# Decoder block on one core: cross-attention's maxima, sums and subtractions in three chains of VectorE instead of one; exponentials placed between product steps; value steps ahead of key steps

## The chip, the cores and the metric

The kernel runs on one core of a Trainium2 chip. Its time is the device time of one execution in microseconds (us). Three executions gave 1714.55, 1710.16 and 1714.2 us, median 1714.2. The engines are named as the profile names them: PE is TensorE (PEld its weight loads), ACT is ScalarE, DVE is VectorE, POOL is GpSimd, SP is SyncE, which issues the DMAs here. Each engine runs its own instructions in the order in which the program issues them, and waits for the others through semaphores.

## The reference

One decoder layer in float32: self-attention, cross-attention to a context of 750 rows, and a gated feed-forward network with quantised weights, each followed by an addition and a layer norm. The change touches the cross-attention alone:

```python
# x: (8, 224, 512), context: (8, 750, 384), 16 heads of 64
q = split_heads(x @ Wq); k = split_heads(context @ Wk); v = split_heads(context @ Wv)
sim = jnp.einsum('bhid,bhjd->bhij', q, k) * SCALE
attn = jax.nn.softmax(sim, axis=-1)          # over the 750 context rows
out = jnp.einsum('bhij,bhjd->bhid', attn, v)
out = out.transpose(0, 2, 1, 3).reshape(b, sq, HEADS * DIM_HEAD) @ Wo + bo
```

The softmax needs, for each head and query, the maximum over 750 scores, the exponentials of the scores less that maximum, and their sum.

## The kernel before

The self-attention fills the first 490 us of the profile or so, the feed-forward network the last 160. Between them the cross-attention runs in 32 **turns** (the loop at line 1408, `for t in range(-1, TURNS)`). A turn is four heads of one batch element. Two batch elements share eight turns: turns 2g and 2g+1 of the eight take the same four heads of the first and of the second element, so query projections come once for two turns, at the end of the odd one. After eight turns the output projection of the two elements follows.

**Layout.** Scores are held transposed: 125 context rows on the partitions, in six tiles (`NCT`), and 224 queries along the free axis. Heads come in two pairs, `w` = 0 and 1; tile `cpT0` or `cpT1` (`pT`) holds the two heads `j` of a pair, 125 x 6 x 224 each. A maximum or a sum over context rows is thus first one over the six tiles, elementwise, and then one across partitions.

**What a turn t issues, in order:**

1. `weighted(t-1)` (line 1326): 48 matmuls, the values of the turn before times its exponentials, into `ov_c`; a copy by ACT to `ov_s`.
2. `reduce_kind(quarter, 1)` (line 1249): DVE reduces `csm`, the partial sums of the exponentials of turn t-1, with a transposing reduction (line 1251).
3. `scores(t)` (line 1211): 48 matmuls (line 1227) into PSUM tiles, 12 copies by ACT to `cpT0`, then `cpT1` (line 1235). As the copies land, DVE takes the maxima over tiles: four tensor-tensor instructions a pair (`cm`, line 1237) and a last one into the region `mx` (line 1241; the profile calls the region by the name of its buffer, `xw`).
4. `across` (line 1256): one chain on DVE for both pairs and for maxima and sums at once. It reduces `mx` (line 1251), copies four partition groups of 32 side by side (`mx_s`, line 1268), reduces to negative maxima (line 1275) and to sums (line 1281), takes the reciprocals of the sums (line 1285) and copies the results to the other partition groups (`mx_n`, three copies, line 1292).
5. `less_maxima(0)` (line 1297): a transposition spreads the negative maxima of pair 0 over the partitions, into the PSUM tile `mx_b` (line 1300); two tensor-tensor instructions, one a head, add them to `cpT0` (line 1307).
6. The projections of the keys for turn t+1 and of the values for turn t, `kv_steps` (line 1167). Each is a generator over `half_steps` (line 1101), which computes the product from seven half-size block products with sums taken beforehand. It has eight steps: PE multiplies, ACT copies the accumulator (a snapshot `m1`, `u2`, `u4`, or a finished block), POOL adds two blocks (lines 1121 and 1140), and in step 7 DVE adds the last (`ckT` or `cv`, line 1148). An accumulator goes on being written after its snapshot is copied. The steps alternate: key 1, value 1, key 2 and so on up to 5; between them stands `weight_work`, the rounding of the feed-forward weights.
7. `exponentials(0)` (line 1316): for each head one ACT instruction (line 1319) and three additions of POOL that sum the six tiles to `csm` (lines 1322 to 1324).
8. Key 6, value 6, `less_maxima(1)`, key 7 and 8, value 7 and 8.
9. `normalise(t-1)` (line 1345): DVE spreads the reciprocals (line 1350) and multiplies `ov_s` into `coT` (line 1360).
10. In odd turns, `query_steps(t+1)` with eight steps of its own; among them `exponentials(1)`, the first head after step 1, the second after step 5.
11. After eight turns, output projections of finished tokens (`mm_co`, line 262) in turns 7, 8, 15, 16, 23, 24 and 31 and behind the loop, transpositions of the next inputs in turns 6, 14 and 22, and sums of the next context by POOL at the ends of turns 6, 7, 14, 15, 22 and 23 (lines 708 and 1074).

The order within each engine is the order of the program text, written out by hand (`manual_schedule`). All tiles named here have one buffer, except `mx_n` with two; PSUM tiles of the tag `mm` have six, handed out in the order in which they came free. SP issues the loads of the blocks of weights and contexts; the change moves none of them.

## Time and profile before

| what | us |
|---|---|
| median of three runs | 1714.2 |
| the profiled execution, whole | 1714.3 |
| its span, first to last instruction | 1712.5 |
| mean granted clock of PE | 0.981 |
| PE idle from 492 to 1556 us of the span (windows over the stage) | 75 |

Turns are read from the trace by the first score product (line 1227) of each. An even turn with neither projection nor transpositions takes 24.8 to 27.2 us (turn 18: 1097.85 to 1122.81, PE busy 24.09 of it). An odd one takes 34.4 to 36.9 (turn 19: 1122.81 to 1157.17, PE busy 30.53), and 29.2 where the turn before held a projection. Eight plain pairs of an even and an odd turn (2-3, 4-5, 10-11, 12-13, 18-19, 20-21, 26-27, 28-29) take 59.1 to 63.0 us, 60.6 on average. The pairs that hold an output projection of two tiles (8-9, 16-17, 24-25) take 66.8 each, and PE is never idle in them.

The page's groups give a line, the engine, the operation, the tile written and those read, the shape, the count, then the time busy and the mean of one in ns, then the engine's idle time just ahead of the group and what ended it. A row of the timeline gives the start and the length in us, the engine, the line, and how often the instruction came in a row.

### The profile page before, as it was taken

How to read it: one execution, taken by the hardware profiler on the slowest of the kernel's cores; microseconds unless marked ns; L12 is line 12 of the kernel's file. 1: busy time of each engine (PE TensorE's matmuls, PEld its weight loads, DVE VectorE, ACT ScalarE, POOL GpSimd, SP SyncE). 2: the span in 40 equal slices, each digit the busy share in tenths (PEclk: the TensorE clock that was granted, in tenths of full speed). 3: DMA queues.
4: the chain of work that ended last, by engine and by line, in shares of the span. 5: the costliest groups of instructions: out<-in, count | busy, mean ns of one | idle time of the engine just before them, and what ended most of it. 6: DMA issues, size and time to landing. Idle time of an engine off the chain costs nothing.

```text
span 1712.5 us, 26691 instructions
## 1 busy us (share of the span) xinstructions
PE 1619.5 (95%) x9682; PEld 1152.9 (67%) x9682; DVE 1339.9 (78%) x2388; ACT 1005.8 (59%) x1874; POOL 962.6 (56%) x861
## 2 busy tenths in 40 slices
PE   8999999999999999989998989988989999989998
PEld 5677666677657777866877756876866877754443
DVE  4999887799937677766678766888986788866877
ACT  5676554566426756745766735766764556545663
POOL 5885566565435646654645674464586456461244
PEclk9999999999999999999999999999999999999999
DMA  8115234243032222321212322322330111112433
GB/s 282 56 61 190 84 122 130 87 128 102 22 134 74 69 69 71 97 89 47 91 55 88 114 83 64 106 85 72 108 109 30 40 35 37 67 50 77 70 82 105
DMA packets 143108, 149.10 MB, mean 87 GB/s; under 512 B 41089, under 2 KB 109185, under 8 KB 142593
## 3 DMA queue, kind: packets, MB, share of 16 engines
q1 hardware_dynamic: 142976, 147.40, 28.3%
q8 instruction: 76, 1.25, 0.3%
q14 instruction: 56, 0.45, 0.1%
HBM read 119.85 MB, written 18.87 MB: 81 GB/s over the span
## 4 chain that ended last, share of the span: by engine, by line
PE 62%; DVE 20%; issue 7%; POOL 6%; ACT 4%; DMA 0%; POOLq 0%; DVEq 0%; SPq 0%; ACTq 0%
PE mm_f L1512 5%; PE mm_co L262 5%; PE ov_c L1335 5%; PE mm_v L544 5%; PE q_x L470 5%; PE mm_o L669 5%; PE sc_c L1227 4%; DVE cpT L1307 4%; DVE cm L1237 3%; PE k_x L1083 3%; POOL csh L1322 3%; PE ov_a L640 3%; PE v_x L1089 3%; PE sc_a L571 3%; PE q_w L470 2%
## 5 line engine op out<-in xcount | busy, mean ns | idle before, releaser
L1322 POOL TENSOR_TENSOR csh<-cpT 125x672 f32<-125x672 f32 x128 | 214.8, 1678 | 92.8 <-DVE cpT L1307 85.7
L1319 ACT ACTIVATE cpT<-cpT 125x1344 f32<-125x1344 f32 x128 | 168.0, 1325 | 97.2 <-DVE cpT L1307 92.5
L200 POOL TENSOR_TENSOR nm_i<-nm_q,mhalf 128x28 f32<-128x28 f32 x32 | 157.9, 4936 | 81.8 <-DVE nm_q L519 81.4
L1307 DVE TENSOR_TENSOR cpT<-cpT,mx_b 125x1344 f32<-125x1344 f32 x128 | 193.2, 1551 | 6.6
L1235 ACT COPY cpT<-sc_c 125x448 f32<-125x448 f32 x384 | 170.6, 592 | 11.5 <-PE sc_c L1227 11.0
L1227 PE MATMUL sc_c<-cq,ckT 64*125 64x224 f32 x1536 | 162.8, 360 | 10.8 <-ACT cpT L1235 10.5
L1227 PEld LDWEIGHTS sc_c<-cq,ckT 64*125 64x125 f32 x1536 | 147.2, 185 | 25.8 <-ACT cpT L1235 12.6
L1335 PE MATMUL ov_c<-cpT,cv 125*64 125x224 f32 x1536 | 155.6, 357 | 7.4 <-DVE cv L1148 7.4
L1121 POOL TENSOR_TENSOR ckT<-ckT,xwq 128x375 f32<-128x375 f32 x32 | 35.5, 1108 | 210.7 <-ACT ckT L1120 210.7
L1335 PEld LDWEIGHTS ov_c<-cpT,cv 125*64 125x64 f32 x1536 | 107.2, 137 | 53.3 <-DVE cv L1148 11.5
L1237 DVE TENSOR_TENSOR cm<-cpT 125x448 f32<-125x448 f32 x128 | 91.9, 759 | 29.3 <-ACT cpT L1235 26.0
L1251 DVE TRANSPOSE_TENSOR_REDUCE mx_r<-csm 128x28 f32<-128x896 f32 x32 | 35.5, 1108 | 91.8 <-POOL csm L1324 91.8
L262 PE MATMUL mm_co<-xattn_Wo,coT 128*128 128x512 f32 x224 | 100.1, 604 | 4.8 <-DVE coT L1360 4.8
L1512 PE MATMUL mm_f<-ternary,xqT 128*128 128x512 bf16 x448 | 98.8, 379 | 1.7 <-DVE x L1373 0.9
L544 PE MATMUL mm_v<-wv,xnT 128*128 128x512 f32 x224 | 100.4, 592 | 0.0
L1096 PE MATMUL mq_x<-xwq 128*128 128x224 f32 x192 | 55.3, 419 | 42.4 <-ACT xwq L1114 41.8
L1323 POOL TENSOR_TENSOR csm<-csh 125x224 f32<-125x224 f32 x128 | 89.0, 696 | 10.0
L282 ACT ACTIVATE pr<-sc_a 128x448 f32<-128x448 f32 x120 | 57.9, 535 | 60.4 <-PE sc_a L571 60.1
L1324 POOL TENSOR_TENSOR csm<-csm,csh 125x224 f32<-125x224 f32 x128 | 85.0, 664 | 10.0
L1237 DVE TENSOR_TENSOR cm<-cpT,cm 125x448 f32<-125x448 f32 x128 | 87.0, 720 | 0.0
L595 DVE TRANSPOSE_TENSOR_REDUCE sm_q<-pr 128x28 f32<-128x896 f32 x64 | 70.6, 1103 | 19.3 <-ACT pr L282 18.9
L1140 POOL TENSOR_TENSOR ckT<-ckT,cku 128x375 f32<-128x375 f32 x32 | 32.6, 1020 | 94.3 <-ACT cku L1139 94.3
(232 smaller groups left out, 3944.9 us busy)
## 6 DMA issues: line engine op xcount, KB each, us to landing
w_slot<-qk_sums SPq DMA_DIRECT2D x22, 512.0 KB, 3.6
xw<-w_sums SPq DMA_DIRECT2D x32, 320.0 KB, 2.9
xwq<-xq_sums SPq DMA_DIRECT2D x16, 512.0 KB, 4.0
w_stage<-w_gateT SPq DMA_DIRECT2D x16, 512.0 KB, 4.5
w_stage<-w_upT SPq DMA_DIRECT2D x16, 512.0 KB, 4.3
w_stage<-w_downT SPq DMA_DIRECT2D x16, 512.0 KB, 3.7
tern<-w_t SPq DMA_DIRECT2D x24, 256.0 KB, 2.5
ternary<-tern SPq DMA_DIRECT2D x3, 2048.0 KB, 7.7
```

Of the source, the lines that this page charges most:

```text
L200: nc.gpsimd.tensor_tensor(y, v, mhalf.to_broadcast([P, v.shape[-1]]), ALU.pow)
L262: nc.tensor.matmul(mm, lhsT=oT[:, k, c : c + P], rhs=w[:, k, :], start=(k == 0), stop=(k == NPAIR - 1),)
L470: nc.tensor.matmul(mm, lhsT=w[:, k], rhs=c[:, k], start=start and k == 0, stop=True, skip_group_check=True,)
L544: nc.tensor.matmul(mm, lhsT=xnT[:, k, at : at + P], rhs=wv[:, k, c * 512 : (c + 1) * 512], start=(k == 0), stop=(k == KD - 1),)
L1227: nc.tensor.matmul(sc[j][:, i, :], lhsT=kT[h0 : h0 + DH, w, ct * CT : (ct + 1) * CT], rhs=q[h0 : h0 + DH, t % 2, w], start=True, stop=True,)
L1235: nc.scalar.copy(pT[:, j, 2 * c2 : 2 * c2 + 2, :], sc[j])
L1237: nc.vector.tensor_tensor(m2[:, j], pT[:, j, 2 * c2 : 2 * c2 + 2, :], pT[:, j, 0:2, :] if c2 == 1 else m2[:, j], ALU.max,)
L1307: nc.vector.tensor_tensor(pT[:, j], pT[:, j], nm[:CT, j] .rearrange("p (o q) -> p o q", o=1) .to_broadcast([CT, NCT, S]), ALU.add,)
L1319: nc.scalar.activation(pT[:, j], pT[:, j], AF.Exp)
L1322: nc.gpsimd.tensor_tensor(half, pT[:, j, 0:3], pT[:, j, 3:6], ALU.add)
L1335: nc.tensor.matmul(ov[h0 : h0 + DH, w, :], lhsT=v[:, ct, hq * DH : (hq + 1) * DH], rhs=pTs[w][:, j, ct, :], start=(ct == 0), stop=(ct == N ...
L1512: nc.tensor.matmul(mm, lhsT=xqTs[i][:, k, :], rhs=w[:, k, cols], start=(k == 0), stop=(k == KD - 1),)
```

## The change

The chain for four heads is taken apart into three: one for the sums (`sum_inverses`), one each for the maxima of pair 0 and of pair 1 (`maxima`). The sums are reduced to their reciprocals right after `weighted`, ahead of the scores. The maxima over tiles leave `scores`; `maxima(pTs[0])` and `less_maxima` of pair 0 come after all scores, then `maxima(pTs[1])`. `mx` shrinks to two heads and serves both pairs. Value steps come ahead of key steps; the exponentials of pair 0 stand after steps 2 and 3 of the two products, ahead of the snapshots of step 3 (`u2`) and of the copies of step 4; `weight_work`'s two middle parts follow step 5. `less_maxima` of pair 1 comes after value step 7 and ahead of key step 7, and the exponentials of pair 1 after value step 8 and after query step 1. The last key step stands ahead of `normalise` in odd turns, and behind the last exponential in even ones.

```diff
@@ -840,8 +840,8 @@
                 n_xw = 2 * (KC + 2 + NSUM) * P
                 xw = xw_all[:, :n_xw].rearrange("p (j i n) -> p j i n", j=2, n=P)
                 bo = xw_all[:, n_xw : n_xw + DIM]
-                mx = xw_all[:, n_xw + DIM : n_xw + DIM + 4 * S].rearrange(
-                    "p (j q) -> p j q", j=4
+                mx = xw_all[:, n_xw + DIM : n_xw + DIM + 2 * S].rearrange(
+                    "p (j q) -> p j q", j=2
                 )
                 open_context(0, ctx_even)
                 load_context(0)
@@ -1214,7 +1214,6 @@
             pTs = []
             for w in range(2):
                 pT = sb.tile([CT, 2, NCT, S], F32, name=f"cpT{w}")
-                m2 = sb.tile([CT, 2, 2, S], F32, name="cm2")
                 for c2 in range(NCT // 2):
                     sc = [
                         ps_mm.tile([CT, 2, S], F32, tag="mm", name=f"sc_c{j}")
@@ -1233,76 +1232,66 @@
                             )
                     for j in range(2):
                         nc.scalar.copy(pT[:, j, 2 * c2 : 2 * c2 + 2, :], sc[j])
-                        if c2 > 0:
-                            nc.vector.tensor_tensor(
-                                m2[:, j], pT[:, j, 2 * c2 : 2 * c2 + 2, :],
-                                pT[:, j, 0:2, :] if c2 == 1 else m2[:, j], ALU.max,
-                            )
-                nc.vector.tensor_tensor(
-                    mx[:CT, 2 * w : 2 * w + 2], m2[:, :, 0, :], m2[:, :, 1, :], ALU.max
-                )
                 pTs.append(pT)
             return pTs
 
-        NH = 4 * NB
-
-        def reduce_kind(quarter, k):
-            y, op = ((mx, ALU.max), (csm, ALU.add))[k]
+        def across(y, n, op, name):
+
+
+            quarter = sb.tile([P, n * NB], F32, name=f"{name}_r")
             nc.vector.tensor_reduce(
-                quarter[:, k], y.rearrange("p j (b c) -> p (j b) c", c=Q32), AX.X, op,
+                quarter, y.rearrange("p j (b c) -> p (j b) c", c=Q32), AX.X, op,
                 apply_transpose=True,
             )
-
-        def across(quarter, first, last):
-
-
-
-
-            kinds = slice(1 if last else 0, 1 if first else 2)
-
-            if not last:
-                reduce_kind(quarter, 0)
-
-            side = sb.tile([Q32, 2, NH, P // Q32], F32, name="mx_s")
+            side = sb.tile([Q32, n * NB, P // Q32], F32, name=f"{name}_s")
             for g in range(P // Q32):
+                nc.vector.tensor_copy(side[:, :, g], quarter[g * Q32 : (g + 1) * Q32])
+            return side
+
+        def sum_inverses():
+
+            side = across(csm, 4, ALU.add, "sm")
+            tot = sb.tile([Q32, 4, NB], F32, name="sm_t")
+            nc.vector.tensor_reduce(
+                tot.rearrange("p j b -> p (j b)"), side, AX.X, ALU.add
+            )
+            res = sb.tile([P, 2, 2, NB, 1], F32, name="sm_n", bufs=2)
+            for j in range(2):
+                nc.vector.reciprocal(res[:Q32, j, :, :, 0], tot[:, j::2])
+            for g in range(1, P // Q32):
                 nc.vector.tensor_copy(
-                    side[:, kinds, :, g], quarter[g * Q32 : (g + 1) * Q32, kinds]
-                )
-
-
-            res = sb.tile([P, 12, NB, 1], F32, name="mx_n", bufs=2)
-            if not last:
-                nc.vector.tensor_reduce(
-                    res[:Q32, 2:6, :, 0].rearrange("p j b -> p (j b)"), side[:, 0], AX.X,
-                    ALU.max, negate=True,
-                )
-            if not first:
-                tot = sb.tile([Q32, 4, NB], F32, name="mx_t")
-                nc.vector.tensor_reduce(
-                    tot.rearrange("p j b -> p (j b)"), side[:, 1], AX.X, ALU.add
-                )
+                    res[g * Q32 : (g + 1) * Q32, g // 2, :, :, 0],
+                    res[:Q32, g // 2, :, :, 0],
+                )
+            return res
+
+        def maxima(pT):
+
+            m2 = sb.tile([CT, 2, 2, S], F32, name="cm2")
+            for c2 in range(1, NCT // 2):
                 for j in range(2):
-                    nc.vector.reciprocal(res[:Q32, 6 * j : 6 * j + 2, :, 0], tot[:, j::2])
+                    nc.vector.tensor_tensor(
+                        m2[:, j], pT[:, j, 2 * c2 : 2 * c2 + 2, :],
+                        pT[:, j, 0:2, :] if c2 == 1 else m2[:, j], ALU.max,
+                    )
+            nc.vector.tensor_tensor(mx[:CT], m2[:, :, 0, :], m2[:, :, 1, :], ALU.max)
+            side = across(mx, 2, ALU.max, "mx")
+            res = sb.tile([P, 2, NB, 1], F32, name="mx_n")
+            nc.vector.tensor_reduce(
+                res[:Q32, :, :, 0].rearrange("p j b -> p (j b)"), side, AX.X, ALU.max,
+                negate=True,
+            )
             for g in range(1, P // Q32):
-                lo, hi = (0, 6) if g == 1 else (2, 8)
-                if first:
-                    lo, hi = 2, 6
-                elif last:
-                    lo, hi = (0, 2) if g == 1 else (6, 8)
-                nc.vector.tensor_copy(
-                    res[g * Q32 : (g + 1) * Q32, lo:hi, :, 0], res[:Q32, lo:hi, :, 0]
-                )
-            return res
-
-        def less_maxima(w, pT, res):
-
+                nc.vector.tensor_copy(res[g * Q32 : (g + 1) * Q32], res[:Q32])
             nm = ps_nm.tile([P, 2, S], F32, name="mx_b")
             nc.vector.transpose(
                 nm.rearrange("p j q -> p (j q)"),
-                res[:, 2 + 2 * w : 4 + 2 * w]
-                .rearrange("p j b o -> p (j b) o")
-                .to_broadcast([P, 2 * NB, Q32]),
-            )
+                res.rearrange("p j b o -> p (j b) o").to_broadcast([P, 2 * NB, Q32]),
+            )
+            return nm
+
+        def less_maxima(nm, pT):
+
             for j in range(2):
                 nc.vector.tensor_tensor(
                     pT[:, j],
@@ -1409,44 +1398,42 @@
             weight_work(t, "open")
             if t >= 1:
                 ov = weighted(t - 1, prior)
+                res = sum_inverses()
             if t >= 0:
-                quarter = sb.tile([P, 2, NH], F32, name="mx_r")
-                if t >= 1:
-                    reduce_kind(quarter, 1)
                 pTs = scores(t)
-                res = across(quarter, t == 0, False)
-                less_maxima(0, pTs[0], res)
+                nm = maxima(pTs[0])
+                less_maxima(nm, pTs[0])
+                nm = maxima(pTs[1])
             ks = kv_steps(t + 1, 0) if t + 1 < TURNS else iter(())
             vals = kv_steps(t, 1) if t >= 0 else iter(())
+            query = query_steps(t + 1) if t % 2 and t + 1 < TURNS else iter(())
             for n in range(5):
+                next(vals, None)
                 next(ks, None)
-                if n in (1, 3):
-                    weight_work(t, ("early", "late")[n // 2])
-                next(vals, None)
-            if t >= 0:
-                exponentials(0, pTs[0])
+                if t >= 0 and n in (1, 2):
+                    exponentials(0, pTs[0], (n - 1,))
+            weight_work(t, "early")
+            weight_work(t, "late")
+            next(vals, None)
             next(ks, None)
             next(vals, None)
             if t == TURNS - 1:
                 normalise(t - 1, ov, res)
             if t >= 0:
-                less_maxima(1, pTs[1], res)
-            for _ in range(2):
+                less_maxima(nm, pTs[1])
+            next(ks, None)
+            next(vals, None)
+            if t >= 0:
+                exponentials(1, pTs[1], (0,))
+            if t < 0 or t % 2:
                 next(ks, None)
-            for _ in range(2):
-                next(vals, None)
             if 1 <= t < TURNS - 1:
                 normalise(t - 1, ov, res)
             prior = pTs
-
-            query = query_steps(t + 1) if t % 2 and t + 1 < TURNS else iter(())
             next(query, None)
             if t >= 0:
-                exponentials(1, pTs[1], (0,))
-            for _ in range(4):
-                next(query, None)
-            if t >= 0:
                 exponentials(1, pTs[1], (1,))
+            next(ks, None)
             for _ in query:
                 pass
             if t % 2 and t + 3 < TURNS:
@@ -1482,9 +1469,7 @@
         last = done[TURNS]
         for i in last:
             cross_project(i, 0, NPAIR - 2)
-        quarter = sb.tile([P, 2, NH], F32, name="mx_r")
-        reduce_kind(quarter, 1)
-        normalise(TURNS - 1, ov, across(quarter, False, True))
+        normalise(TURNS - 1, ov, sum_inverses())
         for i in last:
             cross_project(i, NPAIR - 2, NPAIR)
             cross_add(i)
```

In `normalise` the reciprocals are read as `res[half, j]` in place of `res[half, 6 * j : 6 * j + 2]`.

More of the change, by code (lines that the diff above doesn't have):

```diff
@@ L1254, in reduce_kind @@
             )
-        def across(quarter, first, last):
-            kinds = slice(1 if last else 0, 1 if first else 2)
-            if not last:
-                reduce_kind(quarter, 0)
-            side = sb.tile([Q32, 2, NH, P // Q32], F32, name="mx_s")
-            for g in range(P // Q32):
-                nc.vector.tensor_copy(
-                    side[:, kinds, :, g], quarter[g * Q32 : (g + 1) * Q32, kinds]
-                )
-            res = sb.tile([P, 12, NB, 1], F32, name="mx_n", bufs=2)
-            if not last:
-                nc.vector.tensor_reduce(
-                    res[:Q32, 2:6, :, 0].rearrange("p j b -> p (j b)"), side[:, 0], AX.X,
-                    ALU.max, negate=True,
-                )
-            if not first:
-                tot = sb.tile([Q32, 4, NB], F32, name="mx_t")
-                nc.vector.tensor_reduce(
-                    tot.rearrange("p j b -> p (j b)"), side[:, 1], AX.X, ALU.add
-                )
-                for j in range(2):
-                    nc.vector.reciprocal(res[:Q32, 6 * j : 6 * j + 2, :, 0], tot[:, j::2])
-            for g in range(1, P // Q32):
-                lo, hi = (0, 6) if g == 1 else (2, 8)
-                if first:
-                    lo, hi = 2, 6
-                elif last:
-                    lo, hi = (0, 2) if g == 1 else (6, 8)
-                nc.vector.tensor_copy(
-                    res[g * Q32 : (g + 1) * Q32, lo:hi, :, 0], res[:Q32, lo:hi, :, 0]
-                )
-            return res
@@ new lines, in maxima @@
+        def maxima(pT):
+            m2 = sb.tile([CT, 2, 2, S], F32, name="cm2")
+            for c2 in range(1, NCT // 2):
+                for j in range(2):
+                    nc.vector.tensor_tensor(
[9 more added lines that the diff above has]
+            )
+            for g in range(1, P // Q32):
+                nc.vector.tensor_copy(res[g * Q32 : (g + 1) * Q32], res[:Q32])
@@ L1351, in normalise @@
                     rc[half].rearrange("p w q -> p (w q)"),
-                    res[half, 6 * j : 6 * j + 2]
+                    res[half, j]
                     .rearrange("p w b o -> p (w b) o")
```

## The prediction

> **What bounds the kernel now.** I read the page first, then the list of waits, then each engine's timeline over the cross-attention, turn by turn.
>
> ```profile
> span 1712.5 us, 26691 instructions
> ...
> PE 62%; DVE 20%; issue 7%; POOL 6%; ACT 4%; DMA 0%; POOLq 0%; DVEq 0%; SPq 0%; ACTq 0%
> ```
>
> PE ends most of the chain, DVE a fifth. The change lies in the cross-attention (492 to 1556 us), where PE is idle for 75 us. The waits there form a ring:
>
> ```profile
> ACT cpT L1319 <- DVE cpT L1307: 92.5, 33, 9.0
> DVE mx_r L1251 <- POOL csm L1324: 91.8, 21, 8.3
> POOL csh L1322 <- DVE cpT L1307: 85.7, 30, 9.0
> PE mq_x L1096 <- ACT xwq L1114: 41.8, 11, 6.6
> ```
>
> ACT's exponentials and POOL's sums wait for DVE's subtraction, DVE's next chain waits for POOL's last sum, and PE stands in the query steps because their first snapshot (`xwq`) is queued on ACT behind exponentials. So a plain pair of turns takes 60.6 us on average where PE has 24.1 + 30.5 = 54.6 us of work. DVE's queue in turn 18 (first score product at 1097.85):
>
> ```profile
> 1099.69 1.11 DVE L1251 TRANSPOSE_TENSOR_REDUCE mx_r<-csm 128x28 f32<-128x896 f32 x1 [1.29 <-POOL csm L1324]
> 1100.73 1.12 DVE L1237 TENSOR_TENSOR cm<-cpT 125x448 f32<-125x448 f32 x2
> ...
> 1105.95 0.62 DVE L1241 TENSOR_TENSOR xw<-cm 125x448 f32<-125x448 f32 x1
> ...
> 1111.44 3.02 DVE L1307 TENSOR_TENSOR cpT<-cpT,mx_b 125x1344 f32<-125x1344 f32 x2
> ```
>
> From the sums' reduction to the first subtraction are 11.75 us. The ten maxima take 5.84 us of it (1100.73 to 1106.57) while POOL has nothing to do. Where POOL is busy (turn 15) the same ten take 13.68 (the last line is from POOL's timeline):
>
> ```profile
> 983.04 2.46 DVE L1237 TENSOR_TENSOR cm<-cpT 125x448 f32<-125x448 f32 x2
> 985.42 2.87 DVE L1237 TENSOR_TENSOR cm<-cpT,cm 125x448 f32<-125x448 f32 x2
> 988.33 1.45 DVE L1241 TENSOR_TENSOR xw<-cm 125x448 f32<-125x448 f32 x1
> ...
> 995.44 1.28 DVE L1241 TENSOR_TENSOR xw<-cm 125x448 f32<-125x448 f32 x1
> ...
> 993.54 1.38 POOL L1121 TENSOR_TENSOR cv<-cv,cvm 125x384 f32<-125x384 f32 x1
> ```
>
> Each DVE maximum waits out POOL's instruction in progress, and POOL's next is stretched: `cv` takes 1.38 us there and 0.99 alone. They alternate one to one, at (13.68 - 5.84)/10 = 0.78 us for each DVE instruction. Copies behave likewise (one row of POOL's timeline, one of DVE's):
>
> ```profile
> 1139.88 0.99 POOL L1140 TENSOR_TENSOR cv<-cv,cvu 125x384 f32<-125x384 f32 x1
> ...
> 1139.39 1.72 DVE L1292 COPY mx_n<-mx_n 32x42 f32<-32x42 f32 x3
> ```
>
> Three copies that take 0.56 elsewhere needed 1.72 beside two POOL additions. The subtractions (L1307, one operand in PSUM) always take 1.55, POOL busy or not.
>
> **The parts, on DVE.** Bare costs, from turn 18 and the group means:
> - Sums alone: reduction 1.11, four copies 0.80, reduction 0.25, two reciprocals 0.33, three copies 0.51, gaps 0.2: 3.2 us.
> - Maxima of one pair: four tensor-tensors 2.2, the last 0.65, a half-width reduction (between half of 1.11 and all of it; I take 0.65, since it reads half as much), four copies 0.8, a reduction 0.2, three copies 0.55, transposition 0.75: 5.8.
> - Subtraction of one pair: 3.05, as before.
>
> With `c21` of both products (0.47 each) and `normalise` (2.15) a turn's queue is 3.2 + 2 x 5.8 + 2 x 3.05 + 0.94 + 2.15 = 24.0 us, against 21.1 for the same sum before: three chains instead of one cost 2.9 us bare.
>
> **What moves.** The first subtraction comes 3.2 + 5.8 = 9.0 us after the chain's start instead of 11.75: a gain of 2.75 us for exponentials and sums of pair 0. But `maxima(pTs[1])` now runs right behind `less_maxima(0)`, and that is when POOL starts on pair 0 (in turn 18 `csh` starts 3.1 us after the first subtraction does, as the second ends). The old order had all tensor-tensor maxima at the head of the turn, with POOL idle. POOL then has two heads, (1.62 + 0.66 + 0.66 + 0.2) x 2 = 6.3 us, and two additions of step 5, 2.1 us: 8.4, stretched by 0.37 for each of five tensor-tensors to 10.3. DVE alternates with them to the end: its five tensor-tensors pass in the gaps between the six sums, then the reduction, then copies that meet the two additions. What is left after 10.3 us is two copies, reduction, three copies and transposition, 1.9. So `maxima(1)` takes 12.2 us, not 5.8: contention c = 6.4 us a turn. It was never seen at this place, so bounds: 0, if nothing collides; 12 x 0.78 = 9.4, if all twelve collide. I keep 6.4, near the rows of turn 15 (five at 0.78 are 3.9, the rest longer `csh` and copies).
>
> On which copies collide the Trainium skill has a rule (GPSIMD Engine Reference, section Key points): GpSimd shares its SBUF interfaces with VectorE, with contention for instructions in a two-port mode or with two SBUF inputs. The rows show copies of 32x42 and 32x56 held up, and none of the new 32x14 form beside such an addition. By the rule the small ones collide as well, up to twelve; if only what the rows show collided, c would be the five tensor-tensors, 3.9.
>
> **An even turn**, from its first score product: the first maximum can start when the third copy of scores has landed, 2.55 us (turn 16, 1031.08 to 1033.63). Maxima 5.8, subtraction 3.05, maxima of pair 1 12.2, `c21` of the values 0.47, subtraction 3.05, last exponential 1.4, second half of `ov_c` on PE 2.35: 30.9 us, against 24.8 to 27.2. The last wait is now PE's in `ov_c` for the last exponential. Values first removes the wait of `ov_c` for `cv` (0.77 us in most even turns), which this buries.
>
> **An odd turn.** POOL takes the first head of pair 1 of the turn before at 2.55 + 5.8 + 3.05 + 12.2 + 0.47 + 1.55 + 1.4 = 27.0 us of that turn, and needs 6.3 + 0.4: done 2.8 us into this one. Sums 3.2, maxima 5.8 + 0.8 (one meets the additions of step 2), subtraction 3.05: 15.65. Maxima of pair 1 12.2, `c21` 0.47, first subtraction 1.55, exponential 1.4, the copies of key step 8 and of `xwq` 0.73: 32.0. All that time PE waits for `xwq` (it is out of work at about 24). Then five query products 3.8, `ov_c` 4.7: 40.5, and a slow clock.
>
> A wait of 3.4 us made PE's busy time in odd turns 31.4 (granted clock 0.95) or 32.7 (0.91) instead of 30.5: 0.85 to 2.15 us. I take 1.2, as most such turns lie near the lower one: 41.7 us. The Trainium skill (TensorE: Matmul & The Clock Gate, section HAM oscillation) says that idle stretches beyond some 3.4 us bring half clock; by its 3.4 us of warm-up at half speed the price would be an estimated 1.7, 0.5 more a pair.
>
> A new wait inside: the exponential of head 0 stands on ACT ahead of the `u2` snapshots, so in odd turns those, and PE's step 5 behind them, wait for the subtraction (step 5 is due at 12.4 us, the snapshot lands at 15.8: 3.4 us). The 8 us by which PE waits later hide it; without that cover it costs the 3.4.
>
> **The sum.** A plain pair becomes 30.9 + 41.7 = 72.6 us, 12.0 more. Pairs with a projection: its last two pairs of heads need `coT`, whose `normalise` ends at 27.1 + 0.46 + 2.5 = 30.1 us of the even turn; 20/32 of 13.9 us are left, 8.7, then `ov_c` 4.7: 43.5 (37.6 before). The odd one has no wait for POOL: 2.55 + 5.8 + 3.05 + 12.2 + 0.47 + 1.55 + 1.4 + 0.73 + 3.8 + 1.2 + 4.7 = 37.45 (29.2 before). Together 14.2 more. Pairs with transpositions I price as plain ones. 13 x 12.0 + 3 x 14.2 = 199; the clips of weights (`L989`, 0.69 to 2.1 us, twice a turn in 12 turns) now lie on a full DVE queue, 0.7 a turn: 8. Sum +207 on the span of 1712.5, 1919.5; the median lies 1.7 above the span: **1921 us**. DMAs are not moved; their queue gets more time per turn.
>
> **Rivals.**
> - *No collision, earlier exponentials win* (c = 0; the case on the other side). The pair is 72.6 - 12.8, less 1.2 as PE's wait then stays short: 58.6, 2.0 less than now, x 16 = -32: about 1682. It turns at c = 1.0. For it: the 2.75 us gained and the wait for `cv` gone. Against it: turn 15. Chance 0.07.
> - *They cancel* (c about 1, or slack I don't see): within 0.3%, which is about what can be told from no change here. 0.04.
> - *Half the collision* (c = 3.9): the pair is 5.0 shorter, 67.6, +7.0 x 16 = 112, 1826. For it: small copies were never seen held up. 0.19.
> - *All twelve collide, and DVE's other pieces too* (c = 9.4): +6.0 a pair, 1921 + 96 = 2017. Against it: POOL runs out of work before that. 0.10.
> - Main forecast: 0.60, by itself 1870 to 1975 (c from 5 to 8).
>
> Faster 0.07, same 0.04, slower 0.89. The range, **1822 to 1990**, takes in the half collision and cuts off the first two rivals and most of the last.
>
> **What would show it.** Right: means of L1237's and L1241's successors for pair 1 at 1.2 us or more, copies next to them near 0.6; POOL's `csm` at about 1.0 where it was 0.66; first subtraction 9 us after the sums' reduction; PE waiting 5 us or more in odd turns for `xwq`, and in even ones in the middle of `ov_c`; plain pairs of 70 to 75 us. Wrong: maxima of pair 1 at 0.62 us beside a running `csh`, or pairs at 60 us or below. Then the collision is not what the rows of turn 15 say, and the rest of the sum falls with it.

## The result and the profile after

The changed kernel takes 1924.9 us (median of four runs, 1922.6 to 1926.4) beside 1714.4 for the kernel before: a ratio of 1.123, 95% interval 1.121 to 1.125. The forecast was 1921, with a range of 1822 to 1990. The page of the changed kernel begins, and its chain by engine reads:

```profile
span 1922.1 us, 27094 instructions
...
PE 46%; DVE 33%; ACT 11%; issue 7%; POOL 2%; DMA 0%; POOLq 0%; ACTq 0%; SPq 0%; DVEq 0%
```

DVE's share of the chain went from 20 to 33%, ACT's from 4 to 11%, PE's from 62 to 46%. The table of windows over the cross-attention (length, busy time of each engine with its instructions, the granted clock, the DMA share, GB/s), first of before, then of after, says in what form the time was lost:

```profile
492.00:1556.00 1064.00, 988.54 (x6623) 762.93 (x6622) 812.55 (x1247) 638.36 (x1141) 615.68 (x608) 0.97 0.25 78
```

```profile
490.00:1766.00 1276.00, 1065.49 (x6628) 800.81 (x6627) 1015.22 (x1752) 625.04 (x1141) 642.35 (x608) 0.91 0.21 65
```

The stage is 212 us longer. PE's idle time rose from 75.5 us (1064.00 - 988.54) to 210.5, by 135. The other 77 us are the same matmuls running longer: PE busy 1065.5 for 988.5 at a mean granted clock of 0.91 for 0.97. DVE is busy 203 us longer. The waits of the changed kernel (waiting engine and line, the releaser, us in all, how often, longest):

```profile
ACT cpT L1308 <- DVE cpT L1296: 282.7, 64, 10.2
...
PE mq_x L1096 <- ACT xwq L1114: 79.7, 15, 6.2
...
PE v_x L1089 <- ACT cvu L1129: 55.0, 17, 8.7
...
DVE sm_r L1242 <- POOL csm L1313: 39.4, 14, 5.9
...
PE ov_c L1324 <- DVE cv L1148: 28.0, 10, 2.9
```

POOL no longer holds DVE up at the head of the turn as much (39 us for 92). But ACT's exponentials wait three times as long for DVE's subtractions (283 us for 92), and PE stands behind ACT and DVE above all at three places: `xwq` (80 us for 42), the `u2` snapshot `cvu` (55, new) and `cv` (28 for 7). For the last exponentials it waits 16 us in `ov_c`. DVE's queue in turn 18, which begins at 1212.37, shows why the subtractions are late:

```profile
1211.29 1.10 DVE L1242 TRANSPOSE_TENSOR_REDUCE sm_r<-csm 128x28 f32<-128x896 f32 x1
...
1214.86 1.16 DVE L1273 TENSOR_TENSOR cm<-cpT 125x448 f32<-125x448 f32 x2 [0.46 <-ACT cpT L1234]
1215.94 1.16 DVE L1273 TENSOR_TENSOR cm<-cpT,cm 125x448 f32<-125x448 f32 x2
1217.13 0.63 DVE L1277 TENSOR_TENSOR xw<-cm 125x448 f32<-125x448 f32 x1
...
1218.47 0.72 DVE L1248 COPY mx_s<-mx_r 32x14 f32<-32x14 f32 x4
...
1220.78 3.02 DVE L1296 TENSOR_TENSOR cpT<-cpT,mx_b 125x1344 f32<-125x1344 f32 x2
1223.71 2.58 DVE L1273 TENSOR_TENSOR cm<-cpT 125x448 f32<-125x448 f32 x2
1226.22 2.08 DVE L1273 TENSOR_TENSOR cm<-cpT,cm 125x448 f32<-125x448 f32 x2
1228.33 1.92 DVE L1277 TENSOR_TENSOR xw<-cm 125x448 f32<-125x448 f32 x1
...
1230.97 2.65 DVE L1248 COPY mx_s<-mx_r 32x14 f32<-32x14 f32 x4
...
1234.45 0.66 DVE L1287 STREAM_TRANSPOSE mx_b<-mx_n 128x448 f32<-128x448 f32 x1
1235.14 0.56 DVE L1148 TENSOR_TENSOR cv<-v_w,cvu 125x384 f32<-125x384 f32 x1
```

The same instructions stand there twice. For pair 0 the maxima run from 1214.86 to 1220.68, 5.82 us; for pair 1 from 1223.71 to 1235.11, 11.40, each with the transposition that ends them. The five tensor-tensors take 6.58 us for 2.95, and the four 32x14 copies 2.65 for 0.72. POOL's rows beside them:

```profile
1223.90 1.92 POOL L1311 TENSOR_TENSOR csh<-cpT 125x672 f32<-125x672 f32 x1 [1.06 <-DVE cpT L1296]
1225.89 0.92 POOL L1312 TENSOR_TENSOR csm<-csh 125x224 f32<-125x224 f32 x1
1226.89 0.92 POOL L1313 TENSOR_TENSOR csm<-csm,csh 125x224 f32<-125x224 f32 x1
```

POOL is stretched in turn: `csm` takes 0.92 us where it took 0.66. Over all turns the maxima of pair 1 have a median of 11.38 us. That these sums are the cause is only read off here; the first two experiments test it.

### The profile page after: what moved, and what is told of

The parts are those of the page before. It is cut to its first block, busy times and chain, and to the rows that moved or that the text cites. A ratio compares the mean times of both kernels' runs of the same rounds, so it can differ in the third digit from the quotient of the medians.

```text
span 1922.1 us, 27094 instructions
## 1 busy us (share of the span) xinstructions
PE 1693.7 (88%) x9668; PEld 1189.9 (62%) x9682; DVE 1542.4 (80%) x2893; ACT 992.7 (52%) x1874; POOL 989.4 (51%) x861
## 4 chain that ended last, share of the span: by engine, by line
PE 46%; DVE 33%; ACT 11%; issue 7%; POOL 2%; DMA 0%; POOLq 0%; ACTq 0%; SPq 0%; DVEq 0%
DVE cpT L1296 6%; DVE mx_s L1248 6%; PE ov_c L1324 6%; PE mm_f L1497 5%; ACT cpT L1308 4%; PE mm_co L262 4%; PE mm_v L544 4%; PE q_x L470 4%; PE mm_o L669 4%; DVE xw L1277 4%; DVE cm L1273 4%; PE mq_x L1096 3%; PE sc_c L1226 2%; PE ov_a L640 2%; PE sc_a L571 2%
## 5 line engine op out<-in xcount | busy, mean ns | idle before, releaser
L1324 PE MATMUL ov_c<-cpT,cv 125*64 125x224 f32 x1536 | 190.8, 397 | 44.1 <-DVE cv L1148 28.0
L200 POOL TENSOR_TENSOR nm_i<-nm_q,mhalf 128x28 f32<-128x28 f32 x32 | 158.0, 4937 | 80.8 <-DVE nm_q L519 80.5
L1296 DVE TENSOR_TENSOR cpT<-cpT,mx_b 125x1344 f32<-125x1344 f32 x128 | 192.9, 1549 | 3.3
L1121 POOL TENSOR_TENSOR cv<-cv,cvm 125x384 f32<-125x384 f32 x32 | 32.0, 1001 | 311.1 <-ACT cv L1120 304.2
L1324 PEld LDWEIGHTS ov_c<-cpT,cv 125*64 125x64 f32 x1536 | 119.6, 153 | 116.6 <-DVE cv L1148 32.0
L1226 PE MATMUL sc_c<-cq,ckT 64*125 64x224 f32 x1536 | 158.0, 356 | 4.4 <-ACT cpT L1234 4.1
L1273 DVE TENSOR_TENSOR cm<-cpT 125x448 f32<-125x448 f32 x128 | 124.2, 1012 | 37.2 <-ACT cpT L1234 36.7
L1248 DVE COPY mx_s<-mx_r 32x14 f32<-32x14 f32 x256 | 113.3, 443 | 4.7
L1312 POOL TENSOR_TENSOR csm<-csh 125x224 f32<-125x224 f32 x128 | 111.0, 867 | 10.0
L1089 PE MATMUL v_x<-xw,ctx_odd 128*125 128x128 f32 x480 | 70.1, 290 | 49.4 <-ACT cvu L1129 49.4
L1089 PEld LDWEIGHTS v_x<-xw,ctx_odd 128*125 128x125 f32 x480 | 63.4, 197 | 70.0 <-ACT cvu L1129 57.4
L1273 DVE TENSOR_TENSOR cm<-cpT,cm 125x448 f32<-125x448 f32 x128 | 103.5, 848 | 0.0
L1096 PEld LDWEIGHTS mq_x<-xwq 128*128 128x128 f32 x192 | 47.0, 259 | 89.9 <-ACT xwq L1114 85.1
```

Of the source, the lines that this page charges most:

```text
L1096: nc.tensor.matmul(mm, lhsT=w[:, k], rhs=c[:, k], start=start and k == 0, stop=True, skip_group_check=True,)
L1226: nc.tensor.matmul(sc[j][:, i, :], lhsT=kT[h0 : h0 + DH, w, ct * CT : (ct + 1) * CT], rhs=q[h0 : h0 + DH, t % 2, w], start=True, stop=True,)
L1248: nc.vector.tensor_copy(side[:, :, g], quarter[g * Q32 : (g + 1) * Q32])
L1273: nc.vector.tensor_tensor(m2[:, j], pT[:, j, 2 * c2 : 2 * c2 + 2, :], pT[:, j, 0:2, :] if c2 == 1 else m2[:, j], ALU.max,)
L1296: nc.vector.tensor_tensor(pT[:, j], pT[:, j], nm[:CT, j] .rearrange("p (o q) -> p o q", o=1) .to_broadcast([CT, NCT, S]), ALU.add,)
L1324: nc.tensor.matmul(ov[h0 : h0 + DH, w, :], lhsT=v[:, ct, hq * DH : (hq + 1) * DH], rhs=pTs[w][:, j, ct, :], start=(ct == 0), stop=(ct == N ...
```

## Experiments

In what follows "new" and "old" steps are the orders of the product steps and exponentials after and before the change. Line numbers behind an edit shift by a few: the subtraction L1296 is L1300 where `maxima` was split, for example. Ratios are to the kernel before, with 95% intervals; its median lay between 1710 and 1714 us in the sessions of these runs, so that differences between kernels of a few us say nothing.

**1. POOL's sums of one pair left out.** In the first kernel POOL doesn't sum the exponentials of pair 0, in the second, the control, those of pair 1. Nothing moves.

```diff
-        nc.vector.memset(csm, 0.0)
+        nc.vector.memset(csm, 1.0)
...
                 nc.scalar.activation(pT[:, j], pT[:, j], AF.Exp)
+                if w == 0:
+                    continue
                 half = sb.tile([CT, NCT // 2, S], F32, name="csh")
```

The control has `w == 1` in place of `w == 0`. What was expected of the first:

> The changed kernel without GpSimd's sums of pair 0 (six additions a turn left out, so the sums of those two heads stay at 1; everything else, the exponentials too, is done). Collision theory: the maxima of pair 1 run beside nothing but the two additions of step 5, and shrink from 11.4 us (median, first maximum to the end of the spreading transposition) to 6.3 to 8. Plain pairs of turns fall from 73.5 to some 62 to 63 us, the kernel from 1925 to about 1760. Rival, instructions: three chains cost 2.9 us a turn on VectorE whatever GpSimd does; then the maxima of pair 1 stay as they are and the time stays within 30 us of 1925. Rival, GpSimd's total work: a gain here is the same as where the sums of pair 1 are left out.

And of the control:

> Control: the changed kernel without GpSimd's sums of pair 1, the same six additions a turn, which run beside no maxima. Collision theory: the maxima of pair 1 stay at 11.4 us; what goes is only the wait of the sums' reduction for GpSimd at the head of odd turns (2 to 3 us a pair), so some 1890, a loss against before that remains at over 160 us. Rival, GpSimd's total work is the bound: as fast as without the sums of pair 0 (about 1760).

Without the sums of pair 0: 1748.2 us, ratio 1.022 (1.020 to 1.024), the median of pair 1's maxima 7.02 us. Without those of pair 1: 1887.6 us, ratio 1.104 (1.102 to 1.106), the median still 11.38. The two leave out the same 32 x 2 x 3 instructions. One is worth 177 us, the other 37: it is not POOL's amount of work that counts but where in DVE's queue it falls. The wait of the sums' reduction for `csm` is no part of the 177 us: it is 48.3 us in the first kernel, where it was 39.4. DVE's rows of the first of the two kernels, pair 1 in the turn that begins at 1078.32:

```profile
1091.66 1.16 DVE L1273 TENSOR_TENSOR cm<-cpT 125x448 f32<-125x448 f32 x2
1092.73 1.15 DVE L1273 TENSOR_TENSOR cm<-cpT,cm 125x448 f32<-125x448 f32 x2
1093.92 0.62 DVE L1277 TENSOR_TENSOR xw<-cm 125x448 f32<-125x448 f32 x1
...
1095.26 1.94 DVE L1248 COPY mx_s<-mx_r 32x14 f32<-32x14 f32 x4
```

The tensor-tensors are back at their bare durations. The four copies still take 1.94, as two additions of step 5 fall on them; they were there before the change too.

**2. The same sums, later.** All of the computation is done here; POOL's sums of pair 0 are only issued behind the additions of step 5. The exponentials stay where the change put them.

```diff
                 nc.scalar.activation(pT[:, j], pT[:, j], AF.Exp)
+            if w:
+                sums(w, pT, heads)
+        def sums(w, pT, heads=(0, 1)):
+            for j in heads:
                 half = sb.tile([CT, NCT // 2, S], F32, name="csh")
...
                     exponentials(0, pTs[0], (n - 1,))
+            if t >= 0:
+                sums(0, pTs[0])
             weight_work(t, "early")
```

> The changed kernel with POOL's sums of pair 0 issued behind the additions of step 5 in place of right behind the exponentials; the exponentials stay where they are and the whole computation is done. Theory A (the collision of these sums with the maxima of pair 1 is what the change loses): the maxima of pair 1 take 7 to 9 us in place of 11.4; the sums come 6 us later, so that POOL ends its last sum later too, and part of the gain goes to a longer wait of the sums' reduction for csm at the head of odd turns (3 to 8 us, some 80 in all): 1830 us (1780 to 1870). Theory B (any place of the exponentials ahead of the u2 snapshots sets the turn, the collision is hidden): 1905 to 1930.

1820.3 us, ratio 1.062 (1.060 to 1.064). The median of pair 1's maxima is 8.90 us. DVE's rows in the turn that begins at 1153.07:

```profile
1164.46 1.15 DVE L1273 TENSOR_TENSOR cm<-cpT 125x448 f32<-125x448 f32 x2
1165.53 1.16 DVE L1273 TENSOR_TENSOR cm<-cpT,cm 125x448 f32<-125x448 f32 x2
1166.73 0.63 DVE L1277 TENSOR_TENSOR xw<-cm 125x448 f32<-125x448 f32 x1
...
1168.07 3.31 DVE L1248 COPY mx_s<-mx_r 32x14 f32<-32x14 f32 x4
```

Now the tensor-tensors are free and the copies alone collide, with step 5 and with the first `csh`. The feared wait of the sums' reduction for `csm` hardly moved (42.7 us in all for 39.4), so the theory's price for it was too high; the time lies in the range all the same. From the changed kernel to this one pair 1 loses 11.38 - 8.90 = 2.48 us a turn and the kernel 104.6 us: 42 us of kernel time for each microsecond of collision a turn. The kernel without those sums gives 176.7 / (11.38 - 7.02) = 41, the same slope.

**3. The collision taken away by order.** The chain of pair 1 goes ahead of the subtraction of pair 0, as in the kernel before, and so ahead of POOL's sums. The transposition to `mx_b` becomes a function of its own, `spread`, and `mx_n` gets two buffers. The lines of the loop:

```diff
-                nm = maxima(pTs[0])
-                less_maxima(nm, pTs[0])
-                nm = maxima(pTs[1])
+                negs = [maxima(pT) for pT in pTs]
+                less_maxima(spread(negs[0]), pTs[0])
...
-                less_maxima(nm, pTs[1])
+                less_maxima(spread(negs[1]), pTs[1])
```

> The changed kernel with the chain of maxima of pair 1 moved ahead of the subtraction of pair 0 (only its spreading transposition stays behind). No instruction is added or taken away. Collision theory: the maxima of pair 1 take about 6.4 us instead of 11.4, but the first subtraction comes 5 us later, and with it the exponentials that stand ahead of the u2 snapshots: the wait that the late second subtraction hid (2.3 to 2.8 us in odd turns) grows to 6 to 8 us in every turn and becomes the bound. So only part of the gain shows: about 1885 (1850 to 1910). Rival, the collision is all and the place of the exponentials costs nothing: about 1765. Rival, instruction count: 1925.

1923.7 us, ratio 1.124 (1.122 to 1.126): no gain, and a miss. The collision is indeed all but gone; in the turn shown below both chains and `spread` take 12.1 us together. But the first subtraction now comes 15.3 us behind the sums' reduction in place of 9.5. PE's waits of this kernel, and two rows of ACT's timeline (the turn begins at 1173.02):

```profile
PE v_x L1089 <- ACT cvu L1129: 230.2, 32, 12.7
```

```profile
1190.86 1.32 ACT L1312 ACTIVATE cpT<-cpT 125x1344 f32<-125x1344 f32 x1 [8.33 <-DVE cpT L1300]
1192.09 0.46 ACT L1129 COPY cvu<-v_x 125x384 f32<-125x384 f32 x1
```

ACT is idle for 8.3 us in front of the first exponential, and the `u2` snapshot `cvu`, for which PE waits, stands behind it. PE waits there in every turn, 230 us in all, and for nothing else to speak of. That is 7.2 us a turn, within the 6 to 8 that were expected; what was expected besides, a gain, did not come. From 490 to 1766 us PE is idle for 235.6 us, where it was for 210.5 in the changed kernel. The two waits are substitutes: whether DVE reaches the first subtraction late, or the second, PE stops.

**4. The chains and the steps apart.** First the three chains of the change with the old steps, `less_maxima(nm, pTs[1])` in the old place; then the one chain of before with the new steps. The first, shortened:

```diff
             for n in range(5):
-                next(vals, None)
                 next(ks, None)
-                if t >= 0 and n in (1, 2):
-                    exponentials(0, pTs[0], (n - 1,))
...
+                next(vals, None)
+            if t >= 0:
+                exponentials(0, pTs[0])
             next(ks, None)
             next(vals, None)
...
```

> The three chains of the changed kernel with the step order of before (keys ahead of values, exponentials of pair 0 behind step 5, both subtractions of pair 1 ahead of the additions of step 7). Collision theory: the exponentials wait for step 5, so GpSimd starts on pair 0 later, but the maxima of pair 1 still meet it and the additions of steps 2 and 5; the additions of step 7 (cv, ckT) now wait behind the second subtraction: PE waits for them in the weighted values (8 us or so in even turns) and in the query steps. About 1875 (1830 to 1920). Rival, the loss is due to the new step order (exponentials among snapshots, values first): the old order brings it back to within 20 us of 1714.

The second has the new lines of the loop in the kernel before, with `less_maxima(1, pTs[1], res)`:

> The one chain of before with the whole step order of the change (values first, exponentials of pair 0 ahead of the u2 snapshots and of the copies of step 4). VectorE's maxima all lie at the head of the turn, so nothing collides. Theory of two substitutes: the first subtraction comes 11 to 12 us after the head of VectorE's queue, and PE's step 5 waits 4 to 7 us for u2 in every turn, partly in place of the waits of before: pairs of 66 to 68 us, about 1820 (1790 to 1860). Rival, the collision is the only cost of the change: within 15 us of 1712. Rival, the step order is all of the loss: 1900 or more.

Three chains with old steps: 1833.3 us, ratio 1.071 (1.067 to 1.074). One chain with new steps: 1844.4, ratio 1.077 (1.075 to 1.078). The first lies at the low end of its range. The second is 24 us over its middle, still inside; its wait for the snapshot, 158.0 us in 32 turns, is 4.9 a turn where 4 to 7 were expected. So each half of the change loses by itself, 119 and 130 us, and together they lose 210, less than the sum of 249. PE's waits show two different mechanisms, first those of three chains with old steps, then those of one chain with new steps:

```profile
PE mq_w L1096 <- DVE ckT L1148: 95.9, 15, 10.0
PE ov_c L1324 <- DVE cv L1148: 41.8, 10, 8.4
```

```profile
PE v_x L1089 <- ACT cvu L1129: 158.0, 32, 10.4
```

With the old steps the longer chains make the last additions of the blocks late, `cv` and `ckT` (L1148), which stand in DVE's queue behind both subtractions. This half is not free of the collision: the maxima of pair 1 take 9.82 us there (median), 4.0 more than bare. With the new steps the snapshots stand behind the exponentials. The changed kernel has the longer chains, which show in its waits for `xwq` and `cv`, and the snapshots behind exponentials, and these are eased by the three chains: the wait for `cvu` falls from 158 to 55 us, as the first subtraction comes 9.5 us after the sums' reduction in place of some 12 (11.75 in the kernel before, 11.82 in turn 19 here, 1199.35 to 1211.17).

**5. Chains ahead, old steps, and the sums at two places.** The order of experiment 3 with the old steps; then the same with the chain of the sums moved behind the subtraction of pair 0:

```diff
-                res = sum_inverses()
             if t >= 0:
                 pTs = scores(t)
                 negs = [maxima(pT) for pT in pTs]
                 less_maxima(spread(negs[0]), pTs[0])
+                if t >= 1:
+                    res = sum_inverses()
```

> Three chains with both pairs' maxima ahead of the first subtraction, and the step order of before. Neither the collision nor the exponentials among snapshots: what is left of the change is the number of instructions, 2.9 us a turn on VectorE by the working, plus copies that meet the additions of steps 2 and 5. The first subtraction comes 3 us later than before, and with it the ring of subtraction, exponentials, sums and reduction: some 4 to 6 us a pair, about 1790 (1760 to 1830). Rival, instructions off the critical path cost nothing: 1712.

> Three chains, both maxima chains ahead, the step order of before, and the chain of the sums moved from the head of the turn to behind the subtraction of pair 0. With the sums at the head this kernel took 1821 us. Theory A (what the three chains cost without a collision is the late first subtraction: 3.2 us of sums, and in odd turns the wait for POOL's last sum, stand ahead of it): the first subtraction comes 3 us earlier in even turns and 6 to 8 in odd ones, the wait of the sums' reduction for csm (90 us in all) goes, the waits of PE for xwq (64 us) and in ov_c (40 us) go for the most part: 1725 us (1695 to 1770). Theory B (it is the length of DVE's queue, 24 us of work a turn in place of 21): moving a piece within the queue changes little, 1790 to 1825.

A third kernel is the changed one with the sums between `maxima(pTs[0])` and `less_maxima(nm, pTs[0])`:

> The changed kernel with the chain of the sums moved behind the maxima of pair 0, ahead of the subtraction of pair 0; all else as changed. Theory A (a wait for csm at the head of the chain counts here too): the maxima of pair 0 then cover the wait of 39 us in all, 2.8 us in an odd turn, and the kernel is 1885 us (1865 to 1905). Theory B (the collision and the snapshots behind exponentials set the turn, and POOL's sums of pair 0 begin as late as before): 1912 to 1926. In both, the maxima of pair 1 stay at 11 us.

The first took 1821.4 us, ratio 1.063 (1.062 to 1.065): near the upper end of its range. Without the collision with the sums, and with exponentials behind the snapshots, three chains still cost 107 us. Additions of steps 2 and 5 still hold them up: two chains and `spread` take 13.6 us in turn 17 (1123.75 to 1137.39), where the bare rows of the changed kernel add up to 11.0. How much of the 107 us is this, and how much the number of instructions, was not tried apart. The other two missed by far: 1950.4 (1.136 to 1.142) and 1980.6 (1.155 to 1.160), slower than with the sums at the head. DVE's rows of the second kernel show what the expectations overlooked (its turn begins at 1228.70):

```profile
1231.25 1.16 DVE L1273 TENSOR_TENSOR cm<-cpT 125x448 f32<-125x448 f32 x2 [4.58 <-ACT cpT L1234]
...
1248.32 1.10 DVE L1242 TRANSPOSE_TENSOR_REDUCE sm_r<-csm 128x28 f32<-128x896 f32 x1
1249.46 1.64 DVE L1248 COPY sm_s<-sm_r 32x28 f32<-32x28 f32 x4
...
1251.78 2.26 DVE L1262 COPY sm_n<-sm_n 32x14 f32<-32x14 f32 x3
```

At the head of the turn the sums fill a time in which DVE has to wait for the scores anyhow; with them gone it stands idle there for 4.58 us. Behind the subtraction they lie on the path, and POOL is busy by then: 1248.32 to 1254.04 is 5.7 us, where they take 3.1 at the head (1211.29 to 1214.40 in the changed kernel). `cv` comes that much later: PE waits 7.48 us for it in this turn. Neither theory of that expectation held, and neither reckoned with a chain that grows in its new place. In the third kernel DVE idles at the head likewise (3.19 us in turn 18), and the first subtraction comes 9.66 us after the first maximum (1250.56 to 1260.22) in place of 5.92 (1214.86 to 1220.78); PE's wait for `cvu` grows from 55.0 to 104.8 us.

**6. Values ahead of keys alone, and a late reduction.** Two edits of the kernel before. The first only exchanges key and value steps, the second moves one instruction of 1.1 us, the reduction of `csm`, behind the maxima:

```diff
+                pTs = scores(t)
                 if t >= 1:
                     reduce_kind(quarter, 1)
-                pTs = scores(t)
                 res = across(quarter, t == 0, False)
```

> The kernel before with values ahead of keys at every step and nothing else. It takes away the wait of the weighted values for cv (0.77 us in some ten even turns, 19 us of PE and weight-load idle time together), but puts ckT last, for which the third query product and the transpositions wait. About 1712 (1700 to 1720). If the order of the two products carried the loss, it would be slower by 20 us or more.

> The kernel before with one statement moved: VectorE reduces the sums' partials behind the maxima over tiles, and not ahead of the scores. VectorE then no longer waits for GpSimd's last sum at the head of a turn (91.8 us over the kernel), nor the maxima behind it. If the ring of subtraction, exponentials, sums and reduction sets the odd turns, the first subtraction in them comes 1 to 3 us earlier and the wait of the query steps (1.7 to 3.4 us) shrinks: about 1697 (1685 to 1708). If it doesn't: 1712.

> The kernel before with the sums' reduction behind the scores (1688 us on an earlier chip) and with value steps ahead of key steps. If the wait of ov_c for cv is still there to be removed (0.5 us in even turns) and key blocks cost nothing by coming later: 1680 to 1686. If the wait goes over to mq_w for ckT, as it did with values first alone: 1688 to 1702, no gain.

Values first: 1713.5 us, ratio 1.000 (0.999 to 1.001). The waits of `ov_c` for `cv` become short (0.4 us at most, 2.9 in all for 7.4), and those of `mq_w` for DVE's last additions did not grow (2.8 us for 4.2); that is too little to be seen in the time. The late reduction: **1688.0 us, ratio 0.986 (0.984 to 0.987)**, faster than both kernels and inside the expected range. The longest wait of DVE in it, which was 26.0 us in the kernel before:

```profile
DVE cm L1237 <- ACT cpT L1235: 114.5, 33, 7.4
```

The 92 us for `csm` are gone; DVE waits for scores instead, which it has to have in any case, and in odd turns its maxima no longer stand behind POOL's last sum (in the turn that begins at 1103.94 they start at 1108.59, and the sum ends at 1109.23). PE's wait for `xwq` fell from 41.8 to 28.2 us. Both edits together: 1696.6, ratio 0.991 (0.989 to 0.993), behind the late reduction alone. That is no gain, as the second theory had it, but hardly by the wait it named: `mq_w` waits 3.4 us in all, while the wait for `xwq` is 34.0 us. Why values first costs 9 us here stays open.

## Why the prediction was right, and what of it was not

The mechanism was the one forecast, and the total is 4 us off. But two terms of the sum were wrong by more than that, in opposite directions, so that an agreement this close is luck; what the mechanism by itself bears out is the range.

| step of the prediction | predicted | measured |
|---|---|---|
| sums' reduction to first subtraction, us | 9.0 | 9.49 (1211.29 to 1220.78 in turn 18; median of 31 turns 10.4) |
| chain of the sums, bare | 3.2 | 3.1 |
| maxima of a pair, bare | 5.8 | 5.82 |
| maxima of pair 1 | 12.2 | 11.38 (median of 32) |
| contention c a turn | 6.4 | 5.6 (11.38 - 5.82) |
| plain pair of turns | 72.6 | 73.5 (mean of eight) |
| PE idle in a plain pair | 16.8 (6.8 + 10.0) | 12.7 (4.6 + 8.0) |
| PE busy in a plain pair | 55.8 (54.6 + 1.2) | 60.8 (27.6 + 33.2) |
| pairs with a projection | 81.0 | 83.1 (81.8, 85.2, 82.3) |

**The collision** is shown: taken out of the way with all work kept it is worth 105 us for 2.5 us of it, and leaving out the sums of pair 0 is worth 177. The size of c was high by 0.8. The question left open, whether copies as small as 32x14 collide, is answered: the four take 2.65 us instead of 0.72. The subtractions, with one operand in PSUM, kept their 1.5 us each. The Trainium skill (GPSIMD Engine Reference, Key points) has VectorE and GpSimd share SBUF interfaces, with contention for instructions in a two-port mode or with two SBUF inputs; the tensor-tensors here have two, and whether the copies run in a two-port mode no run shows. The lower bound of 3.9, tensor-tensors alone, was too low: they cost 3.6 in turn 18 and the copies 1.9 more.

**The rival on the other side**, no collision and 1682 us, turned at c = 1.0 by the forecast. No run had c = 0 with the first subtraction as early as in the change; experiment 3 comes near to c = 0, but pays with a later subtraction. By the measured slope, the kernel with later sums would reach 1820 - 3.1 x 42 = 1690 without the rest of its collision; that is a line drawn on, not a run. The sum itself had 2 x 16 = 32 us for each microsecond of c, too little beside 41 to 42. Part of the rest is the clock: over the stage it is 0.95 in the kernel with later sums and 0.91 in the changed one.

**The clock** is the term that was mis-sized, and it makes up for the difference. It stood at 1.2 us in an odd turn, the price of a wait of 3.4 us, where the sum itself had PE wait for some 8. In an even turn it stood at nothing, with no reason given, where the sum had PE idle for 6.8. Measured, PE's busy time in a plain pair is 60.8 us where the rows of full clock have 54.6: 6.2, five times as much, 3.5 of it in the even turn. By the clock records of the traces PE ran at half clock for 229 us of the stage, where before it did for 61. The 167 us more can cost half their length, 84; the 77 us by which PE's busy time grew lie near that. Turn 19 shows it in PE's timeline:

```profile
1254.10 1.47 PE L1089 MATMUL v_w<-xw,ctx_odd 128*125 128x128 f32 x12
...
1259.61 1.04 PE L1089 MATMUL v_x<-xw,ctx_odd 128*125 128x128 f32 x6 [2.77 <-ACT cvu L1129]
1260.44 1.46 PE L1083 MATMUL k_x<-ctx_even,xw 128*128 128x375 f32 x2
1261.69 2.47 PE L1089 MATMUL v_w<-xw,ctx_odd 128*125 128x128 f32 x12
...
1268.59 0.92 PE L1096 MATMUL mq_z<-xT,xwq 128*128 128x224 f32 x4
1274.66 1.86 PE L1096 MATMUL mq_x<-xwq 128*128 128x224 f32 x4 [5.15 <-ACT xwq L1114]
1276.31 1.70 PE L1096 MATMUL mq_w<-xwq 128*128 128x224 f32 x4
```

There are two stalls in the turn, and behind each the same shapes run longer: twelve products of `v_w` 2.47 us instead of 1.47, four query products 1.86 and 1.70 instead of 0.92. The prediction priced one. In turn 18 the clock is 0.59 from 1235.7 to 1244.1, behind the stall of 2.90 us. The prediction also had PE's wait for `xwq` end 32.0 us into the odd turn, which is 30.6 here (1274.66 - 1244.02), and the rest of the turn then took 11.7 us where it had 9.7. That is how two errors met in a turn of 42.3 us for 41.7. Over the eight pairs an odd turn took 41.3 us, and an even one 32.2 for 30.9.

**The new wait** behind the exponentials, in odd turns, was forecast at 3.4 us, hidden by PE's later one; it is 2.77 in turn 19 and 1.0 to 2.8 in all plain odd turns. In turns 7, 15 and 23 it is 6.6 to 8.7; the prediction priced their pairs as plain. The end of the later wait is indeed set by DVE's queue. What was missed is that the step order could cost 130 us alone, as it does where the first subtraction comes later (experiment 4).

**The even turn** was to wait in the middle of `ov_c` for the last exponential alone, and values first to bury the wait for `cv`. In turn 18 PE waits first 2.90 us for `cv`, whose last addition (L1148) DVE reaches at 1235.14 behind the maxima of pair 1, and then 0.94 and 0.46 for exponentials. The cause is the same queue.

**The clips of weights**, 8 us in the sum, were not tried apart. In the traces the four plain pairs without clips (2-3, 4-5, 26-27, 28-29) rose by 12.05 us on average, from 60.39 to 72.44, and the four with clips by 13.7, from 60.8 to 74.5. That fits a price for clips, but is no test of it. Nor was the granted clock tried apart: no run removed the slow rows and kept the waits.

## What to carry to other kernels

When a chain is cut up to let another engine start earlier, look at what that engine will do while the rest of the chain runs: here POOL's additions doubled the time of the maxima behind them, and the same additions a few microseconds later gave half the loss back. Fill the time in which an engine must wait anyway with work that nobody waits for, and move no more than the instruction that blocks: in the kernel before, one reduction of 1.1 us moved behind the maxima gained 1.5%; in the kernel with three chains ahead, a whole chain of 3.1 us moved behind the subtraction lost 7%. Price a stall of PE with the slow rows that can follow it, and each stall by itself.

## What the hardware showed beyond that

A stall's length alone did not tell whether slow rows followed. In the kernel of three chains with old steps PE waited 3.41 us in the middle of `ov_c`, and the 36 products behind it ran at full clock:

```profile
1190.90 3.63 PE L1324 MATMUL ov_c<-cpT,cv 125*64 125x224 f32 x36 [3.41 <-DVE cv L1148]
```

That is the 3.63 us of the same 36 in the kernel before, behind a wait of 0.87. In the changed kernel 2.77 us were enough for a granted clock of 0.61 from 1259.6 to 1264.0. The Trainium skill (TensorE: Matmul & The Clock Gate, HAM oscillation) puts the bound at idle gaps over some 3.4 us; here 2.77 us lie below it and brought slow rows, and 3.41 lie at it and brought none.

The clock records of the traces tell the two apart. They hold two values only, 1.0 and 0.5, and the clock changes only on a grid. Around turn 19 it does so at 1236.374, 1243.201, 1260.268, 1263.681, 1273.921 and 1280.748 us, which lie 2, 5, 1, 3 and 2 steps of 3.413 us apart. Here are windows on this grid (length, busy time of PE, PEld, DVE, ACT and POOL, the granted clock, the DMA share, GB/s), first two of the changed kernel, then two of the other:

```profile
1256.86:1260.27 3.41, 0.66 (x6) 0.66 (x7) 3.41 (x4) 2.40 (x4) 0.94 (x1) 1.00 0.00 0
1260.27:1263.68 3.41, 3.41 (x15) 2.62 (x14) 3.41 (x3) 3.41 (x7) 3.18 (x4) 0.50 0.00 0
```

```profile
1185.81:1189.22 3.41, 1.68 (x16) 0.97 (x14) 3.27 (x4) 1.15 (x2) 3.18 (x4) 1.00 0.13 38
1189.22:1192.63 3.41, 1.73 (x18) 1.35 (x20) 3.37 (x6) 1.99 (x2) 2.48 (x4) 1.00 0.00 0
```

The 2.77 us fell into one window and left PE busy for 0.66 us of it; the next window ran at half clock. The 3.41 us fell across two windows and left PE busy for half of each; the clock stayed full. All fourteen traces, cut like this from 495 us on, agree. Of the windows at full clock, all 334 in which PE was busy for less than 0.41 of the time were followed by half clock, and all 4342 with more than 0.55 by full clock; in between both occur. At half clock PE had to be busy for over 0.8 of a window before full clock came back: in turn 18 2.33 us of 3.41 were not enough, 3.11 were. So it is the share of a window that a stall takes which decides in these traces. Where the grid lies in a run was not known ahead, and so a stall of this size has to be priced both ways.
